# Spectral mixing matmuls of one frequency on 128x32 tiles instead of two frequencies on 128x64 tiles

## The chip, the cores and the metric

The kernel runs on one core of a Trainium2 chip. The metric is the device time of one execution in microseconds (us), as the median of several runs. One further execution was recorded by the hardware profiler; all views of the profile come from it. Engines are named as the profile names them: PE is TensorE (matmuls), PEld its weight loads, DVE VectorE, ACT ScalarE, POOL GpSimd, SP SyncE, which here only issues DMAs.

## The reference

The input x has 16 images of 16 channels of 256x256 numbers in fp32. Two layers are applied, each as "normalise in groups, convolve, add to the input":

```python
x = x + _L0_conv_ref(_gn(x), L0_conv_weight)
x = x + _L1_conv_ref(_gn(x), L1_conv_ty, ..., L1_conv_weights_residue)
```

The first convolution is a circular 3x3 convolution, written with FFTs. The second is a Laplace layer:

```python
alpha = jnp.fft.fft2(x, axes=(-2, -1))
S = jnp.einsum('ikpq,oikp,xikq->oxik', weights_residue, A, Bm)
output_residue1 = jnp.einsum('biox,oxik->bkox', alpha, S)
...
x1 = jnp.fft.ifft2(output_residue1, s=(Ny, Nx), axes=(-2, -1)).real
return x1 + x2 / Nx / Ny
```

S holds, for each of the 256x256 frequencies, a complex 16x16 matrix from input channel i to output channel k. The second einsum mixes the channels with it, frequency by frequency, for all 16 images b. It is this einsum that the change touches. x2, a transient part, is made of a few projections of alpha and of exponentials.

## The kernel before

Everything is fp32. The span has four stages, each with its own pools of SBUF and PSUM tiles, and in each the program order of every engine's instructions is the order in which the Python code issues them (a manual schedule); semaphores keep the data dependencies between engines.

1. To about 640 us: the 3x3 convolution with 32x32 tiles of the PE array (`conv`, L300); its result, folded in y, goes to vD in HBM.
2. To about 1195 us: the transform along y and x by matmuls with cosine and sine tables (L786, L794, L829), and projections (L814). The spectrum goes to aD in HBM: 128 x-frequencies on the first axis, 32 rows (16 channels, real and imaginary), then 256 y-frequencies by 16 images.
3. From 1206 to 1797 us: the mixing stage, which the change touches.
4. From there to the end: the inverse transform, per output channel k and group of four images (L1398 along x, L1422 and L1423 along y), the addition of the input, and the store of the result.

**The mixing stage.** The loop at L1242 takes 32 rounds g of four x-frequencies each. A round has four quarters n (also called jq) of 64 y-frequencies. A moving tile `abd[jq]` holds the spectrum of the four x-frequencies s as a block-diagonal operand: its 128 partitions are 32 rows times four s, and outside the blocks it is zero (memset once; `load`, L1115, writes only the blocks). So one matmul over 128 partitions mixes four x-frequencies at once, and 64 of its columns (four s by 16 images b) belong to one y-frequency. There is one `abd` buffer per quarter, quarters 0 and 1 sharing a tile that one `load` call fills (four DMAs of 256 KB); quarters 2 and 3 take four DMAs of 128 KB each.

The stationary operand `sg` holds S for the round: 128 partitions, 128 pairs of y-frequencies, 32 outputs m (16 channels, real and imaginary), and the two members e of the pair. It is made one round ahead: `sums` (L1036) forms it with matmuls on 64x32 tiles from the weights of `weights` (L904: DVE and POOL), and `spread` (L1060) copies it from PSUM, half of it by an ACT copy, half by a DVE shuffle.

`mix` (L1132) handles 16 y-frequencies per call. One matmul (L1141) takes a pair of them at once: the stationary operand has 64 columns (32 m by 2 e), the moving one 128 columns (2 frequencies o by 4 s by 16 b). The product holds all four combinations of e and o; only those with e = o are wanted. Two column tiles t of 64 columns are used, one for each half of the y-frequencies. A call fills one PSUM tile `ps_mix` (512 columns, one bank, four buffers), which is copied whole to the row tile `yt` (L1265), by ACT for m = 0 and 1, and by DVE for m = 3; m = 2 goes to DVE just after a step of `make_exps` in which ACT loads a table, otherwise to ACT.

A quarter's `yt` (three buffers) is written to yD in HBM by `store` (L1153) in two DMAs, one per e, which pick the wanted half. yD has, for each x-frequency, 64 rows (t and m) of 2048 numbers (e, quarter, then image and frequency), with a gap of 256 numbers after each row. All loads and stores of this stage are issued by SP in program order: per quarter `store(g, n)` and `load(g + 1, n)`, where for n = 1 the load comes first. `make_exps` (L1182) spreads the making of the exponentials for stage 4, mostly POOL work, over the quarters. After round 30, `unmix_first` (L1160) reads back the part of yD with x-frequency 0, separates two frequencies that share it and writes it again.

**The start of stage 4.** `load_images` (L1315) reads the channel-0 part of yD, four images at a time (the first on the POOL queue for 120 partitions and on SP for the last 8; the rest on SP); `load_quarter` (L1337) reads the later channels in quarters, one row of 2048 numbers for each partition. `combine` (L1350, POOL) then forms the operand of the inverse transform.

Of the kernel before, what the change touches and what calls it, by code (L numbers as in the profile page):

```python
# [9 lines left out]
FP = mybir.dt.float32  # L10
# [14 lines left out]
def conv_then_laplace_kernel(ctx: ExitStack, tc: tile.TileContext, a: dict, out: bass.AP):  # L25
# [44 lines left out]
        t = dp.tile([P, C, 8 * N + 256], FP, name=f"vD{b}", tag=f"vD{b}")  # L70
        vD.append(t[:, :, 0 : 8 * N].rearrange("p c (b h x) -> p c b h x", b=4, h=2))
    aD = pitched("aD", 2 * C, N * B)
    yD = pitched("yD", 4 * C, N * B // 2, 2, 4)
    cD = dp.tile([P, 4, 8, N], FP, name="cD", tag="cD")
    hD = dp.tile([7, 2, 16, C * C * 4], FP, name="hD", tag="hD")
    eD = [dp.tile([n, P, C, 2, P], FP, name=f"eD{n}", tag=f"eD{n}") for n in (2, 1)]
# [917 lines left out]
    ptab.close()  # L994


    yp = pool(p2, "yt", 3)
    g0 = pool(p2, "sg0")
    a0 = pool(p2, "abd0")
    wp = pool(p2, "w", 2)  # L1000
# [128 lines left out]
                    out=abd[jq][s::4, s].rearrange("r c j b -> r c (j b)"), in_=src[:, :, jq]  # L1129
                )  # L1130

    def mix(n, sg, yt):  # L1132


        ps = pm.tile([P, 4, 2, 4, B], FP, name="ps_mix", tag="ps_mix")
        jq = n // 4
        for j in range(4):
            cc, jj = divmod(4 * (n % 4) + j, 8)
            for t in range(2):
                f = 128 * t + 64 * cc + 16 * jq + 2 * jj  # L1140
                nc.tensor.matmul(  # L1141
                    ps[64 * t : 64 * t + 64, j],
                    lhsT=sg[:, f // 2].rearrange("p m e -> p (m e)"),
                    rhs=abd[jq][:, :, 2 * t + cc, 2 * jj : 2 * jj + 2].rearrange(
                        "p s j b -> p j s b"
                    ),
                    start=True,
                    stop=True,
                )
        j0 = 4 * (n % 4)  # L1150
        return yt[:, :, :, j0 : j0 + 4], ps.rearrange("p j o s b -> p o (s b) j")

    def store(g, jq, yt):  # L1153
        for e in range(2):
            nc.sync.dma_start(
                out=yD[4 * g : 4 * g + 4, :, e, jq].rearrange("s k n -> k s n"),
                in_=yt[e::2, e].rearrange("p (s b) j -> p s (b j)", s=4),
            )

    def unmix_first():  # L1160

        z2 = new_sg(32).rearrange("p (a n) m e -> p a (n m e)", a=4)[:, 0:2]
        z, t = (z2[:, j, 0:1024].rearrange("p (c n) -> p c n", c=4) for j in range(2))
        at = yD[0]
        for c in range(4):
            nc.sync.dma_start(out=z[:, c], in_=at[32 * (c // 2) : 32 * (c // 2) + 32, c % 2])
        yield
        lo, hi = z[:, 0:2], z[:, 2:4]  # L1170
        nc.vector.scalar_tensor_tensor(t[:, 0:2], hi, osgn, lo, ALU.mult, ALU.add)
        nc.vector.scalar_tensor_tensor(t[:, 2:4], lo, nosgn, hi, ALU.mult, ALU.add)
        nc.vector.tensor_scalar(t, t, 0.5, None, ALU.mult)
        t0, z0 = t[:, 0:3:2, 0:256:16], z[:, 0:3:2, 0:256:16]
        nc.vector.tensor_tensor(z0, z0, t0, ALU.subtract)
        nc.vector.scalar_tensor_tensor(t0, z0, first, t0, ALU.mult, ALU.add)
        for c in range(4):
            nc.sync.dma_start(out=at[32 * (c // 2) : 32 * (c // 2) + 32, c % 2], in_=t[:, c])

    def make_exps(which):  # L1182


        pl = ep.tile([P, C, 2], FP, name="s_pl", tag="s_pl")
        nc.sync.dma_start(out=pl, in_=a[f"pole_e{which + 1}"])
        t = ep.tile([P, N], FP, name="s_t", tag="s_t")
        nc.sync.dma_start(out=t, in_=a[("ty", "tx")[which]].to_broadcast([P, N]))
        most, least = (cols[:, j : j + 1] for j in ((8, 10), (11, 18))[which])
        sign, phase, turns = (cols[:, 2 + 3 * which + j : 3 + 3 * which + j] for j in range(3))  # L1190
        pim = ep.tile([P, C], FP, name="s_pim", tag="s_pim")
        for _ in range(4):
            yield
        nc.gpsimd.tensor_scalar(pim, pl[:, :, 1], sign, None, ALU.mult)
        for q in range(8):
            th = ep.tile([P, 2, N], FP, name="s_th", tag="s_th")
            rn = ep.tile([P, N], FP, name="s_rn", tag="s_rn")
            tmp = ep.tile([P, N], FP, name="s_tmp", tag="s_tmp")
            ex = ep.tile([P, 2, N], FP, name="s_ex", tag="s_ex")
            for j in range(2):  # L1200
                i = 2 * q + j
                nc.gpsimd.tensor_scalar(th[:, j], t, pim[:, i : i + 1], None, ALU.mult)
            magic = 1.5 * 2.0**23
            c1 = 6.28125
            c2 = float(np.float32(1.93500518798828125e-3))
            c3 = 2 * np.pi - c1 - c2
            for j in range(2):
                z = th[:, j]
                nc.gpsimd.tensor_scalar(rn, z, 1.0 / (2 * PI), turns, ALU.mult, ALU.add)
                nc.gpsimd.tensor_scalar(rn, rn, magic, magic, ALU.add, ALU.subtract)  # L1210
                for c in (c1, c2, c3):
                    nc.gpsimd.tensor_scalar(tmp, rn, float(c), None, ALU.mult)
                    nc.gpsimd.tensor_tensor(z, z, tmp, ALU.subtract)
                yield
            nc.gpsimd.tensor_scalar(th, th, most, least, ALU.min, ALU.max)
            for j in range(2):
                i = 2 * q + j
                nc.scalar.activation(ex[:, j], t, AF.Exp, scale=pl[:, i, 0:1])
            yield True
            yield  # L1220
            nc.scalar.activation(th, th, AF.Sin, bias=phase)
            yield True
            nc.gpsimd.tensor_tensor(th, th, ex, ALU.mult)
            for op, eo in ((ALU.add, 0), (ALU.subtract, 1)):
                nc.gpsimd.tensor_tensor(
                    ex[:, :, eo * P : eo * P + P], th[:, :, 0:P], th[:, :, N - 1 : P - 1 : -1], op
                )
            yield
            for o in range(2 - which):
                nc.sync.dma_start(  # L1230
                    out=eD[which][o, :, 2 * q : 2 * q + 2].rearrange("p i e t -> p i (e t)"),
                    in_=ex,
                )
            yield
# [3 lines left out]
    ahead, wt = first_sums(), None  # L1238
    o2 = finish_projections()
    unmix = None  # L1240
    exps, late = chain(make_exps(0), make_exps(1)), None
    for g in range(32):  # L1242
        sg, w_now = ahead, wt
        if g == 0:
            w_now = at_once(weights(1))
            nc.gpsimd.memset(abd[3], 0.0)
            steps = weights(2)
            next(steps)
        ahead = new_sg(g + 1) if g < 31 else None
        for n in range(4):  # L1250
            if g == 0:
                sets = ((), (0,), (1,), (2, 3))[n]
            else:
                sets = (n,) if ahead is not None else ()
            if g == 0:
                banks = {j: sums(j, w_now) for j in sets}
            elif sets and n % 2 == 0:
                banks = {j: sums(j, w_now) for j in (n, n + 1)}
            evict = [banks[j] for j in sets]
            yt = yp.tile([P, 2, 4 * B, 16], FP, name="yt", tag="yt")  # L1260
            for m in range(4):
                for j, ps in zip(sets, evict) if m < 2 else ():
                    spread(j, (ahead, [couples(z) for z in ps]), odds=(m,))
                o, src = mix(4 * n + m, sg, yt)
                (nc.vector.tensor_copy if m >= (2 if late else 3) else nc.scalar.copy)(o, src)  # L1265
            if n == 1 and g < 31:
                load(g + 1, n)
            store(g, n, yt)
            if g == 0 and n == 0:
                load(0, 3)  # L1270
            if n != 1 and g < 31:
                load(g + 1, n)
            if n == 1 and unmix is not None:
                next(unmix, None)
            if n == 3:
                steps = weights(g + 3) if g < 29 else iter(())
            wt = next_step(steps, None) or wt
            late = g and next(exps, None)
        if g == 30:
            unmix = unmix_first()  # L1280
            next(unmix)
# [33 lines left out]
    def load_images(yk, b0, rows, eng):  # L1315

        at = slice(16 * b0, 16 * b0 + 64)
        for r in range(2):
            for h in range(2):
                eng.dma_start(  # L1320
                    out=yk[r][rows, h].rearrange("p c b j -> p c (b j)")[:, :, at],
                    in_=yD[rows, 2 * C * h + C * r].rearrange("p e q n -> p (e q) n")[:, :, at],
                )

    def load_tables(k, eng=nc.gpsimd):
# [11 lines left out]
    def load_quarter(k, n, yk):  # L1337
        r, h = divmod(n, 2)
        nc.sync.dma_start(
            out=yk[r][:, h].rearrange("p c b j -> p (c b j)"),  # L1340
            in_=yD[:, 2 * C * h + C * r + at(k)].rearrange("p e q n -> p (e q n)"),
        )

    def load_v(k, b0):
# [305 lines left out]
```

## Time and profile before

| What | Value |
|---|---|
| Median of 3 runs | 2562.41 us (2560.56 to 2570.66) |
| Profiled execution, its own time | 2559.74 us |
| Its span | 2557.7 us, 83730 instructions |
| Mean granted TensorE clock | 0.99 |
| PE busy | 2446.8 us (96%), 35314 matmul records |
| DVE busy | 1836.5 us (72%) |
| ACT busy | 1433.9 us (56%) |
| POOL busy | 1255.0 us (49%) |
| DMA | 653.11 MB, mean 255 GB/s |

The span is what the profiler saw from the first to the last instruction; the execution's time is 2.0 us longer. Busy shares are averages over four stages with different limits, so a stage has to be read by itself. A group of instructions is given as line, engine, operation, output and inputs, tile of the PE array (rows*columns), shape, count, then the busy time in us, the mean duration of one in ns, and the idle time of the engine just before them with what ended it. An fp32 matmul appears as two records on PE and two on PEld. Records of matmuls that run in different tiles of the array overlap, so busy time (their union) is far below count times mean. Matmul ends are modelled; their starts are recorded.

### The profile page before, as it was taken

The page shows a single profiled execution, that of the slowest core. Times are in us where ns is not written, and L with a number is a line of the kernel's source. Part 1 is how long each engine was busy: PE and PEld are TensorE (multiplying, and loading weights), DVE is VectorE, ACT ScalarE, POOL GpSimd, SP SyncE. Part 2 cuts the span into 40 slices and gives each one's busy share as a digit, 9 for nine tenths or more (in the row PEclk, how much of TensorE's full clock was granted, in tenths as well). Part 3 has the DMA queues.
Part 4 walks back from the last instruction along what each step waited for, and adds up shares of the span by engine and source line. Part 5 has one row for each costly group of instructions (what it writes and reads, how often), then busy time and mean ns, then how long its engine had stood idle before and what let it go on. Part 6 is the DMA issues. An engine that isn't in the chain of part 4 may idle for free. (4 is left out here: it accounts for less than half of the span.)

```text
span 2557.7 us, 83730 instructions
## 1 busy us (share of the span) xinstructions
PE 2446.8 (96%) x35314; PEld 1895.7 (74%) x35314; DVE 1836.5 (72%) x3771; ACT 1433.9 (56%) x2603; POOL 1255.0 (49%) x1277
## 2 busy tenths in 40 slices
PE   4999999999999999998999999999899999999998
PEld 2454555457777777775899999998688888888887
DVE  7777789848888888887566666665367676666766
ACT  2566666675666666665677767776344434444443
POOL 1333369442333333334376756664655655556553
PEclk9999999999999999999999999999899999999999
DMA  7889878865456456456777777777988888889884
GB/s 272 271 292 300 280 264 292 289 239 201 189 224 247 194 218 247 194 219 216 230 255 248 255 253 246 243 244 247 278 286 292 293 291 283 294 282 306 282 290 167
DMA packets 314070, 653.11 MB, mean 255 GB/s; under 512 B 45238, under 2 KB 160054, under 8 KB 301792
## 3 DMA queue, kind: packets, MB, share of 16 engines
q1 hardware_dynamic: 312720, 644.23, 73.2%
q8 instruction: 278, 4.55, 0.7%
q0 software_dynamic: 928, 3.02, 0.5%
q10 hardware_dynamic: 48, 0.52, 0.2%
q14 instruction: 96, 0.79, 0.1%
HBM read 368.15 MB, written 280.36 MB: 254 GB/s over the span
## 5 line engine op out<-in xcount | busy, mean ns | idle before, releaser
L1362 POOL TENSOR_TENSOR u<-yk 128x512 f32<-128x512 f32 (+1 forms) x268 | 351.7, 1345 | 313.8 <-PE ps_p L1398 243.9
L300 PE MATMUL ps_conv<-xt,wc 32*32 32x512 f32 x12288 | 447.2, 606 | 30.5 <-issue 21.0
L1141 PEld LDWEIGHTS ps_mix<-abd,sg 128*64 128x64 f32 x8192 | 446.8, 137 | 36.7 <-issue 30.0
L1141 PE MATMUL ps_mix<-abd,sg 128*64 128x128 f32 x8192 | 463.4, 274 | 9.2 <-DVE yt L1265 4.9
L300 PEld LDWEIGHTS ps_conv<-xt,wc 32*32 32x32 f32 x12288 | 252.3, 104 | 212.5 <-issue 117.7
L802 ACT ACTIVATE t<-ps_y,vmr 128x384 f32<-128x384 f32 x512 | 296.8, 580 | 156.6 <-PE ps_y L794 156.4
L786 PE MATMUL ps_y<-tabE,vq 128*128 128x256 f32 x1024 | 313.3, 388 | 1.8 <-ACT t L802 1.8
L794 PE MATMUL ps_y<-tabO,vq 128*128 128x256 f32 x1024 | 305.9, 380 | 0.0
L1422 PE MATMUL ps_f<-pt,inv 128*128 128x256 f32 x1008 | 300.5, 380 | 0.0
L1423 PE MATMUL ps_f<-hs,ey 128*128 128x256 f32 x1008 | 299.8, 379 | 0.0
L271 POOL TENSOR_TENSOR pair<-pair,far 128x1024 f32<-128x1024 f32 x64 | 151.7, 2370 | 297.2 <-DVE pair L268 195.5
L1398 PEld LDWEIGHTS ps_p<-inv,u 128*128 128x128 f32 x2048 | 268.6, 193 | 35.3 <-POOL u L1366 11.4
L1398 PE MATMUL ps_p<-inv,u 128*128 128x128 f32 x2048 | 276.2, 278 | 9.9 <-POOL u L1366 9.8
L1426 DVE TENSOR_TENSOR r<-ps_f,q 128x256 f32<-128x256 f32 x256 | 106.9, 418 | 245.0 <-ACT q L1425 224.1
L1265 ACT COPY yt<-ps_mix 128x512 f32<-128x512 f32 x352 | 203.2, 586 | 110.6 <-PE ps_mix L1141 39.4
L1425 ACT COPY q<-ps_f 128x256 f32<-128x256 f32 x256 | 95.4, 372 | 273.9 <-PE ps_f L1423 250.4
L786 PEld LDWEIGHTS ps_y<-tabE,vq 128*128 128x128 f32 x1024 | 189.5, 191 | 78.6 <-ACT q L842 50.3
L1265 DVE COPY yt<-ps_mix 128x512 f32<-128x512 f32 x160 | 108.9, 688 | 180.8 <-PE ps_mix L1141 175.4
L1400 ACT COPY pt<-ps_p 128x512 f32<-128x512 f32 x256 | 151.5, 592 | 137.1 <-PE ps_p L1398 137.1
L666 POOL TENSOR_TENSOR vq<-vf 128x512 f32<-128x512 f32 x63 | 80.1, 1272 | 289.8 <-DVE vf L670 278.8
L1066 ACT ACTIVATE sg<-ps_s,mcol 128x512 f32<-128x512 f32 (+1 forms) x264 | 178.5, 677 | 68.8 <-PE ps_s L1043 30.0
L794 PEld LDWEIGHTS ps_y<-tabO,vq 128*128 128x128 f32 x1024 | 195.5, 191 | 26.8
(243 smaller groups left out, 4037.0 us busy)
## 6 DMA issues: line engine op xcount, KB each, us to landing
xt<-in_x SPq DMA_DIRECT2D x288, 258.0 KB
vD<-pair SPq DMA_DIRECT2D x256, 256.0 KB
yD<-yt SPq DMA_DIRECT2D x256, 256.0 KB
vl<-vD SPq DMA_DIRECT2D x128, 512.0 KB
out_y<-ol SPq DMA_DIRECT2D x128, 512.0 KB
s<-vD SPq DMA_DIRECT2D x124, 512.0 KB
aD<-spec SPq DMA_DIRECT2D x15, 4096.0 KB
yk<-yD SPq DMA_DIRECT2D x60, 1024.0 KB
```

Of the source, the lines that this page charges most:

```text
L271: nc.gpsimd.tensor_tensor(lo, lo, hi, ALU.subtract)
L300: nc.tensor.matmul(acc[r][32 * c : 32 * c + 32], lhsT=ready[b][0][rows, phase, tap], rhs=halves[b][u // 2][rows, q : q + 5 : 4, 2 - tap : ...
L786: nc.tensor.matmul(ps[:, 0:N], lhsT=vf[:, xo, 0, j], rhs=tabE[:, 0 : i + 2 : i + 1], start=True, stop=False, skip_group_check=True,)
L794: nc.tensor.matmul(ps[:, P : P + N], lhsT=vf[:, xo, 1, j], rhs=tabO[:, i : C + 1 : C - i], start=False, stop=True, skip_group_check=True,)
L802: nc.scalar.activation(t[:, xo, j].rearrange("p l n -> p (l n)"), ps[:, 0:384], AF.Copy, scale=vmr[:, 0, b0 + j, i : i + 1],)
L1066: nc.scalar.activation(columns_of(to, k), src[odd], AF.Copy, scale=nsgn)
L1141: nc.tensor.matmul(ps[64 * t : 64 * t + 64, j], lhsT=sg[:, f // 2].rearrange("p m e -> p (m e)"), rhs=abd[jq][:, :, 2 * t + cc, 2 * jj : 2 ...
L1265: (nc.vector.tensor_copy if m >= (2 if late else 3) else nc.scalar.copy)(o, src)
L1362: nc.gpsimd.tensor_tensor(u[:, :, j].rearrange("p b (c n) -> p c b n", c=8), in0, in1, o)
L1398: nc.tensor.matmul(ps[:, at], lhsT=u[:, n], rhs=tab, start=True, stop=True)
L1422: nc.tensor.matmul(ps[:, e], lhsT=tab, rhs=pt[:, e], start=True, stop=False)
L1423: nc.tensor.matmul(ps[:, e], lhsT=ey[:, e], rhs=hs, start=False, stop=True)
```

## The change

Each mixing matmul takes one y-frequency: 32 stationary columns (the m of one e, every second number of `sg`), 64 moving columns, and one of four column tiles c = (t, e) of 32 columns. Every product is wanted. There are twice as many matmuls, each with half the columns in both operands. A call of `mix` now covers 32 y-frequencies in one PSUM tile of 512 columns, so there are two calls a quarter instead of four. ACT copies the first, DVE the second; the flag that moved a copy to DVE is gone. `yt` is half as large and has six buffers; one `store` of 128 partitions writes it. yD has 128 rows (c and m) of 1024 numbers (quarter, image, frequency) with the same gap of 256. The readers of yD follow: `load_images` has four DMAs for each of two parts where it had two, `load_quarter` reads two pieces of 1024 numbers for each partition, and `unmix_first` addresses the new rows. Block-diagonal operands, `sums`, `spread`, the loads of `abd` and the order of loads and stores stay.

```diff
-    yD = pitched("yD", 4 * C, N * B // 2, 2, 4)
+    yD = pitched("yD", 8 * C, N * B // 4, 1, 4)[:, :, 0]
...
-    yp = pool(p2, "yt", 3)
+    yp = pool(p2, "yt", 6)
...
-    def mix(n, sg, yt):
-        ps = pm.tile([P, 4, 2, 4, B], FP, name="ps_mix", tag="ps_mix")
-        jq = n // 4
-        for j in range(4):
-            cc, jj = divmod(4 * (n % 4) + j, 8)
-            for t in range(2):
-                f = 128 * t + 64 * cc + 16 * jq + 2 * jj
+    def mix(n, cc, sg, yt):
+        ps = pm.tile([P, 8, 4, B], FP, name="ps_mix", tag="ps_mix")
+        for j in range(8):
+            for c in range(4):
+                t, e = divmod(c, 2)
                 nc.tensor.matmul(
-                    ps[64 * t : 64 * t + 64, j],
-                    lhsT=sg[:, f // 2].rearrange("p m e -> p (m e)"),
-                    rhs=abd[jq][:, :, 2 * t + cc, 2 * jj : 2 * jj + 2].rearrange(
-                        "p s j b -> p j s b"
-                    ),
+                    ps[32 * c : 32 * c + 32, j],
+                    lhsT=sg[:, 64 * t + 32 * cc + 8 * n + j, :, e],
+                    rhs=abd[n][:, :, 2 * t + cc, 2 * j + e],
                     start=True,
                     stop=True,
                 )
-        j0 = 4 * (n % 4)
-        return yt[:, :, :, j0 : j0 + 4], ps.rearrange("p j o s b -> p o (s b) j")
+        return yt[:, :, 8 * cc : 8 * cc + 8], ps.rearrange("p j s b -> p (s b) j")

     def store(g, jq, yt):
-        for e in range(2):
-            nc.sync.dma_start(
-                out=yD[4 * g : 4 * g + 4, :, e, jq].rearrange("s k n -> k s n"),
-                in_=yt[e::2, e].rearrange("p (s b) j -> p s (b j)", s=4),
-            )
+        nc.sync.dma_start(
+            out=yD[4 * g : 4 * g + 4, :, jq].rearrange("s k n -> k s n"),
+            in_=yt.rearrange("p (s b) j -> p s (b j)", s=4),
+        )
...
-            yt = yp.tile([P, 2, 4 * B, 16], FP, name="yt", tag="yt")
-            for m in range(4):
-                for j, ps in zip(sets, evict) if m < 2 else ():
+            yt = yp.tile([P, 4 * B, 16], FP, name="yt", tag="yt")
+            for m in range(2):
+                for j, ps in zip(sets, evict):
                     spread(j, (ahead, [couples(z) for z in ps]), odds=(m,))
-                o, src = mix(4 * n + m, sg, yt)
-                (nc.vector.tensor_copy if m >= (2 if late else 3) else nc.scalar.copy)(o, src)
+                o, src = mix(n, m, sg, yt)
+                (nc.vector.tensor_copy if m else nc.scalar.copy)(o, src)
...
-            for h in range(2):
+            for c in range(4):
+                h, e = divmod(c, 2)
                 eng.dma_start(
-                    out=yk[r][rows, h].rearrange("p c b j -> p c (b j)")[:, :, at],
-                    in_=yD[rows, 2 * C * h + C * r].rearrange("p e q n -> p (e q) n")[:, :, at],
+                    out=yk[r][rows, h, 4 * e : 4 * e + 4].rearrange("p c b j -> p c (b j)")[:, :, at],
+                    in_=yD[rows, 2 * C * c + C * r][:, :, at],
                 )
...
         nc.sync.dma_start(
-            out=yk[r][:, h].rearrange("p c b j -> p (c b j)"),
-            in_=yD[:, 2 * C * h + C * r + at(k)].rearrange("p e q n -> p (e q n)"),
+            out=yk[r][:, h].rearrange("p (e c) b j -> p e (c b j)", e=2),
+            in_=yD[:, 4 * C * h + C * r + at(k) :: 2 * C][:, 0:2].rearrange("p e q n -> p e (q n)"),
         )
```

More of the change, by code (lines that the diff above doesn't have):

```diff
@@ L1167, in unmix_first @@
         for c in range(4):
-            nc.sync.dma_start(out=z[:, c], in_=at[32 * (c // 2) : 32 * (c // 2) + 32, c % 2])
+            nc.sync.dma_start(out=z[:, c], in_=at[32 * c : 32 * c + 32])
         yield
@@ L1177, in unmix_first @@
         for c in range(4):
-            nc.sync.dma_start(out=at[32 * (c // 2) : 32 * (c // 2) + 32, c % 2], in_=t[:, c])
+            nc.sync.dma_start(out=at[32 * c : 32 * c + 32], in_=t[:, c])
     def make_exps(which):
@@ L1218, in make_exps @@
                 nc.scalar.activation(ex[:, j], t, AF.Exp, scale=pl[:, i, 0:1])
-            yield True
+            yield
             yield
             nc.scalar.activation(th, th, AF.Sin, bias=phase)
-            yield True
+            yield
             nc.gpsimd.tensor_tensor(th, th, ex, ALU.mult)
@@ L1240, in conv_then_laplace_kernel @@
     unmix = None
-    exps, late = chain(make_exps(0), make_exps(1)), None
+    exps = chain(make_exps(0), make_exps(1))
     for g in range(32):
@@ L1277, in conv_then_laplace_kernel @@
             wt = next_step(steps, None) or wt
-            late = g and next(exps, None)
+            if g:
+                next(exps, None)
         if g == 30:
```

## The prediction

> **What bounds the kernel now.** I read the 40 slices first, then the costliest groups, then the time line of TensorE through one round of the mixing stage, then the engines' windows. The changed code runs from 1206 to 1797 us, slices 19 to 28.
>
> The page, busy tenths in 40 slices of 64 us:
>
> ```profile
> PE   4999999999999999998999999999899999999998
> ...
> DMA  7889878865456456456777777777988888889884
> ```
>
> TensorE is full all through, the stage of interest included; the DMA engines stand at seven tenths there. Next the groups (line, engine, operation, count, then busy us, mean ns, idle before):
>
> ```profile
> L1141 PE MATMUL ps_mix<-abd,sg 128*64 128x128 f32 x8192 | 463.4, 274 | 9.2 <-DVE yt L1265 4.9 <-issue 2.3 <-DMA abd<-aD 1.6
> L300 PE MATMUL ps_conv<-xt,wc 32*32 32x512 f32 x12288 | 447.2, 606 | 30.5 <-issue 21.0 <-ACT pair L319 5.7 <-DVE wc L244 3.7
> ...
> L1265 ACT COPY yt<-ps_mix 128x512 f32<-128x512 f32 x352 | 203.2, 586 | 110.6 <-PE ps_mix L1141 39.4 <-ACT sg L1066 24.8 <-DMA abd<-aD 21.6
> ...
> L1265 DVE COPY yt<-ps_mix 128x512 f32<-128x512 f32 x160 | 108.9, 688 | 180.8 <-PE ps_mix L1141 175.4 <-issue 2.1 <-DMA yD<-yt 1.6
> ...
> L1382 PE MATMUL ps_h<-et,o 32*32 32x256 f32 x2048 | 55.4, 392 | 4.7 <-DVE r L1427 4.7
> ...
> L814 PE MATMUL psd<-t,hB 128*32 128x128 f32 x1024 | 42.9, 279 | 0.3 <-ACT t L802 0.3
> ```
>
> The mixing matmuls idle 9 us in 463, and the copies wait for them, not they for the copies. One fp32 matmul is two records: 4096 matmuls, 8192 rows. The time line of TensorE (start, length) gives one round g:
>
> ```profile
> 1240.87 1.96 PE L1043 MATMUL ps_s<-ct,w 64*32 64x256 f32 x64
> 1242.76 7.21 PE L1141 MATMUL ps_mix<-abd,sg 128*64 128x128 f32 x128
> 1249.89 1.96 PE L1043 MATMUL ps_s<-ct,w 64*32 64x256 f32 x64
> 1251.78 7.21 PE L1141 MATMUL ps_mix<-abd,sg 128*64 128x128 f32 x128
> 1258.92 0.88 PE L1043 MATMUL ps_s<-ct,w 64*32 64x256 f32 x24
> ```
>
> A round is 1258.92 - 1240.87 = 18.05 us with no gap: twice 1.88 us of sums and 7.14 us of mixing (55.8 ns a record). The windows of that stage (us, then busy us and instructions of PE, PEld, DVE, ACT, POOL, then clock, DMA share, GB/s):
>
> ```profile
> 1400.00:1500.00 100.00, 100.00 (x2128) 90.12 (x2126) 65.45 (x163) 73.15 (x121) 67.68 (x75) 1.00 0.79 253
> ```
>
> So TensorE is the bound. Behind it, per round: DMA 14.0 us at its mean share of 0.775, ACT 13, POOL 12, DVE 11.8.
>
> [...] matmul records in different column tiles start 6 to 14 ns apart. [...] the mixing stage moves 248 on average and 370 in its busiest 4 us.
>
> **The mixing matmuls.** Now a pair of column tiles streams 128 columns and takes 2 x 55.8 = 111.6 ns. After, four column tiles stream 64 columns each, twice as many matmuls (8192, 16384 records). If streaming sets the pace, a group of four takes half the pair's time, 56 ns, or 14 ns a record: 16384 x 14 = 229 us for 463. Weights need not slow it: a load record takes 190 ns for 128 columns, 137 for 64, 106 for 32, so 27 ns per 32 columns over a constant, and loads of different column tiles overlap. Line 814 is the same tile shape with 128 columns: in one burst its records start at 0, 13, 26, 40, 133, 146, 160, 173, 242 ns, so four per 109 ns, all four tiles at full speed.
>
> What no row shows for long is the rate of instructions: four per matmul (two loads, two matmuls), so one per 7 ns. The nearest is a burst of line 1382 that had just waited (PE, then PEld, of that line alone):
>
> ```profile
> 2522.28:2522.53 0.25, 0.25 (x30) 0.24 (x28) 1.00 0.93 377
> ```
>
> 58 instructions in 0.25 us are 4.3 ns each, a matmul per 17 ns. The other end is line 300, where records come every 447.2 / 12288 = 36.4 ns; but 512 columns on 16 tiles need 26.7 of that for streaming, and its PSUM and ACT waits are in it. Bounds: 14 to 36 ns a record; I take 14 to 15, since the burst shows the supply and line 814 the tiles. TensorE's round becomes 2 x (1.88 + 256 x 14 ns) = 2 x 5.46 = 10.9 us.
>
> **What takes over.** Copies: 512 become 256, 128 on each engine. ACT loses 224 x 586 ns = 131 us, DVE 32 x 688 = 22 us; both have slack today, so this is worth nothing by itself, but leaves ACT 9 and DVE 11.2 us a round. POOL keeps its 11.8. SP: a round issues 12 loads and 8 stores at 0.60 us, 12.1 us; after, 12 and 4, some 9.7 us (a 128-row store at 0.6; if it took 1.2, 12.1). Bytes are unchanged, 4.19 MB a round besides the tables, so DMA keeps 14.0 us of work and becomes the longest. abd has one buffer: quarters 0 and 1 (1 MB) are loaded once mixing of quarter 1 ends, needing some 2.4 us of issue, 3.3 of transfer, and queueing; yet the other stores and loads of the round are issued without waiting for that load, so the engines have about 8 us of work queued when it lands, against 3.7 us until the next is issued. DMA can run without a hole. At 4.19 + 0.25 MB and 300 to 370 GB/s the round is 12.0 to 14.8 us; I take **14.2 us**. Gain in 30 steady rounds: 30 x (18.05 - 14.2) = 115.5 us.
>
> Round 0 (1206.3 to 1240.9) has 14.6 us of mixing among waits for POOL, ACT and loads: half of the 7 us saved, 4 us. Round 31 ends through the unmixing of frequency 0 (a load, five DVE operations, four stores, with the last yD stores behind them on SP). The 4.95 us for which TensorE waits there on a copy go with six yt tiles, but SP's chain stays: 1 us.
>
> **The last stage.** Its start is exposed: the stores land at 1799.5 us, then the first images are read through four POOL issues (0.93 us each for 960 pieces; 128-piece ones take 0.54) and SP. Eight of half the pieces take about 0.70 each: +1.9 us; SP's first group doubles from 1.34 us, and 12 further issues become 24: they took 1.6 us each with 1024 pieces, held by the queue, so pieces, not counts, set them. I take **+3 us** (bounds 0 and 10). Then quarters of yk arrive in 4 KB pieces for 8 KB ones. In this trace a 4 KB piece takes 174 ns and an 8 KB one 454, so it costs nothing, and TensorE covers it (496.6 of 500 us busy); without that cover 60 loads would show a few us at most. The steadier alternation of copies and the dropped flag around the table loads cost ACT at most a wait that four PSUM banks hide.
>
> Sum, against the profiled execution: 2559.7 - 115.5 - 4 - 1 + 3 = 2442 us. The median of the runs shown is 2.7 us above that execution, so I predict 2445.
>
> **Rivals.**
> 1. *Instruction supply sets the pace* (slower). Twice the records at line 300's 36.4 ns: 16384 x 36.4 = 596 us against 463, so about 2695 us. It decides from 463.4 / 16384 = 28.3 ns a record on. For it: no row of the page is below 27 ns a record (line 1382: 55.4 / 2048), and instructions are fetched by the same DMA engines that I expect to be full. Against: the burst, and that those rows hold short bursts with their tails.
> 2. *A floor in between.* [...] about 2515. The same comes out if [...] the single abd buffer leaves holes in the queue.
> 3. *DMA is no bound.* TensorE, DVE and POOL at about 11.8 us: 30 x 6.25 = 188 us, about 2375.
> 4. *Hidden anyway*: excluded as long as TensorE is full; it comes back only as an exact tie of 1 or 2 with today, 2550 to 2575.
>
> **Chances.** My forecast 0.50 (its own range 2405 to 2485), rival 2 0.16, rival 3 0.09, a tie 0.05, rival 1 0.20. So 0.75 faster, 0.05 within 0.5% (13 us, about what a measurement of this kernel can tell from no change), 0.20 slower. The range reaches from half of rival 3 to the near edge of rival 1: 2385 to 2600.
>
> **What would show it.** Right: 16384 mixing records at 14 to 18 ns each while they run; rounds of about 14 us; TensorE below full in slices 19 to 26, its idle time ended by abd<-aD; DMA share near 1, around 300 GB/s or more; 128 copies each on ACT and DVE; the last stage's 46 us steps unchanged. Wrong: TensorE still full with mixing above 500 us (rival 1); rounds of 16 to 17 us [...] (rival 2); DMA share below 0.85 while TensorE waits for abd (holes); the first images of the last stage later by over 10 us after the last yD store.

## The result, and the profile after

The changed kernel takes 2669.28 us (median of 5 runs, 2664.34 to 2675.37); the kernel before, run beside it, 2561.17 us (2555.77 to 2570.66). The ratio is 1.042, with a 95% interval of 1.039 to 1.045. The forecast of 2445 us and its range were wrong, and so was the sign: what came is rival 1, that the supply of instructions sets the pace.

The page after: engines and DMA in 40 slices of 67 us (busy tenths, then GB/s), then the DMA queue that carries instructions (packets, MB, share of 16 engines). The mixing stage lies in slices 18 to 28.

```profile
PE   5999999989999999996666666666699999999998
...
DMA  7888888755565556546666666666888888888884
GB/s 268 274 292 292 286 275 306 263 212 202 195 253 230 197 206 245 226 173 226 201 209 213 214 213 204 205 217 200 221 319 291 293 296 284 285 293 286 301 283 177
...
q8 instruction: 343, 5.62, 0.9%
```

TensorE is no longer full in the stage, at six or seven tenths, and the DMA engines, which the forecast had made the new bound, are less busy than before: about 210 GB/s for 250. Both engines that were to be the bound wait.

The costliest groups of TensorE and the copies after, every shape by itself (line, engine, operation, tile, shape, count, then busy us, mean ns, idle before with what ended it):

```profile
L300 PE MATMUL ps_conv<-xt,wc 32*32 32x512 f32 x12288 | 450.1, 603 | 29.8 <-issue 22.1 <-DVE wc L244 3.7 <-ACT pair L319 3.6
...
L1139 PE MATMUL ps_mix<-abd,sg 128*32 128x64 f32 x16384 | 306.8, 235 | 214.8 <-issue 211.2 <-DMA abd<-aD 3.3 <-DVE sg L1098 0.2
...
L1259 ACT COPY yt<-ps_mix 128x512 f32<-128x512 f32 x128 | 75.0, 586 | 275.4 <-PE ps_mix L1139 182.5 <-issue 85.8 <-DMA abd<-aD 4.9
L1259 DVE COPY yt<-ps_mix 128x512 f32<-128x512 f32 x128 | 88.4, 691 | 292.2 <-PE ps_mix L1139 289.6 <-DMA abd<-aD 2.2
```

The mixing matmuls are busy for 307 us, 157 less than before, and stand still for 215 where they stood 9. 211 of these are put down to "issue": nothing that the profile shows was awaited, neither data (3.3 us for abd) nor a free PSUM bank. The time line of TensorE in one stretch of the stage (start, length, count, idle before) gives this a shape:

```profile
1500.82 2.00 PE L1139 MATMUL ps_mix<-abd,sg 128*32 128x64 f32 x128 [0.99 <-issue]
1504.29 0.98 PE L1139 MATMUL ps_mix<-abd,sg 128*32 128x64 f32 x52 [1.48 <-issue]
1505.19 1.96 PE L1043 MATMUL ps_s<-ct,w 64*32 64x256 f32 x64
1507.08 0.36 PE L1139 MATMUL ps_mix<-abd,sg 128*32 128x64 f32 x9
1508.02 2.00 PE L1139 MATMUL ps_mix<-abd,sg 128*32 128x64 f32 x127 [0.58 <-issue]
1512.85 1.89 PE L1139 MATMUL ps_mix<-abd,sg 128*32 128x64 f32 x120 [2.83 <-issue]
```

While they run, the matmuls are as fast as forecast: 128 records in 2.00 us, of which the last takes 0.22, so 14.0 ns from record to record. Then TensorE stops for 0.6 to 2.8 us. From stop to stop it runs some 128 records: 52 + 64 + 9 = 125 is about the same count across two kinds of matmul. With the weight loads, as many records again, and the semaphore instructions among them, that is 256 instructions: of the 98 distances between the 99 stops over 0.6 us from 1260 to 1800 us, 96 are 256, 512 or 768 instructions exactly.

The engines' windows in that stage say the same (us, then busy us and instructions of PE, PEld, DVE, ACT, POOL, then clock, DMA share, GB/s):

```profile
1400.00:1500.00 100.00, 65.26 (x2912) 51.73 (x2900) 49.25 (x125) 41.41 (x65) 57.56 (x66) 0.90 0.67 215
```

5812 TensorE instructions in 100 us, for 4254 before: 17.2 ns each. The faster matmuls bought a third more instructions in the same time, but the change needs 1280 a round where there were 768, two thirds more.

Where the time went, by stages of the two profiled executions (their spans differ by 104.9 us): mixing from its first to its last matmul takes 698.3 us for 587.4, 110.9 more; from there to the end 760.0 for 764.0, 4 less; what lies before, 2 less.

### The profile page after: what moved, and what is told of

It is laid out like the page before. It is cut to its first block, busy times and chain, and to the rows that moved or that the text cites. A ratio compares the mean times of both kernels' runs of the same rounds, so it can differ in the third digit from the quotient of the medians.

```text
span 2662.6 us, 99892 instructions
## 1 busy us (share of the span) xinstructions
PE 2327.6 (87%) x43506; PEld 1731.6 (65%) x43506; DVE 1816.0 (68%) x3739; ACT 1320.5 (50%) x2379; POOL 1265.4 (48%) x1281
## 4 chain that ended last, share of the span: by engine, by line
PE 75%; issue 10%; DVE 7%; DMA 6%; SPq 2%; ACT 1%; POOL 1%; DVEq 0%; ACTq 0%; POOLq 0%
PE ps_mix L1139 11%; PE ps_conv L300 10%; PE ps_y L786 9%; PE ps_y L794 8%; PE ps_p L1394 7%; PE ps_f L1418 7%; PE ps_f L1419 7%; PE ps_s L1043 6%; PE ps_x L829 4%; PE ps_h L1378 2%; DMA vD<-pair 2%; PE psd L814 1%; DMA xt<-in_x 1%; DVE r L1427 1%; DVE ol L1429 1%
## 5 line engine op out<-in xcount | busy, mean ns | idle before, releaser
L1358 POOL TENSOR_TENSOR u<-yk 128x512 f32<-128x512 f32 (+1 forms) x268 | 358.2, 1370 | 299.5 <-PE ps_p L1394 238.7
L1139 PE MATMUL ps_mix<-abd,sg 128*32 128x64 f32 x16384 | 306.8, 235 | 214.8 <-issue 211.2
L1139 PEld LDWEIGHTS ps_mix<-abd,sg 128*32 128x32 f32 x16384 | 275.5, 120 | 263.7 <-issue 260.1
L1259 DVE COPY yt<-ps_mix 128x512 f32<-128x512 f32 x128 | 88.4, 691 | 292.2 <-PE ps_mix L1139 289.6
L1066 ACT ACTIVATE sg<-ps_s,mcol 128x512 f32<-128x512 f32 (+1 forms) x264 | 173.0, 675 | 129.8 <-PE ps_s L1043 100.1
L1259 ACT COPY yt<-ps_mix 128x512 f32<-128x512 f32 x128 | 75.0, 586 | 275.4 <-PE ps_mix L1139 182.5
```

Of the source, the lines that this page charges most:

```text
L1066: nc.scalar.activation(columns_of(to, k), src[odd], AF.Copy, scale=nsgn)
L1139: nc.tensor.matmul(ps[32 * c : 32 * c + 32, j], lhsT=sg[:, 64 * t + 32 * cc + 8 * n + j, :, e], rhs=abd[n][:, :, 2 * t + cc, 2 * j + e], s ...
L1259: (nc.vector.tensor_copy if m else nc.scalar.copy)(o, src)
L1358: nc.gpsimd.tensor_tensor(u[:, :, j].rearrange("p b (c n) -> p c b n", c=8), in0, in1, o)
```

## What the stops are

The queue q8 carries 343 packets of 16.4 KB; before it carried 278 (0.7% of the 16 engines' span). TensorE's matmuls and weight loads are 2 x 43506 after and 2 x 35314 before, 254 to a packet both times, and with its semaphore and drain instructions the trace has 87964 and 71342, 256 to 257 to a packet. So the packets of q8 hold blocks of 256 TensorE instructions, and their times in the trace's DMA records can be set beside the stops. The DMA view of the 400 us from 1300 to 1700, kernel before:

```profile
q8 instruction: 67, 1.10, 1.1%
```

and after:

```profile
q8 instruction: 93, 1.52, 1.6%
```

Before, a block lasts 5.97 us on average; after, 4.30 us. Five blocks of 4.30 us are the 21.5 us of a round after (178 copies of sg, eight a round, in 480 us: 21.6 us). In the DMA records of the changed kernel, a block lands, and TensorE goes on 1.39 us later (median of the 99 stops; eight of ten lie between 1.26 and 1.55). The next fetch starts 1.48 us after that (median, most between 1.1 and 2.7), and takes 1.0 us. The medians add up to some 3.9 us from block to block, and 99 of 100 fetches of the stage start at least 3.37 us after the one before. Counted on in steps of 256 instructions, TensorE enters 93 blocks from 1300 to 1700 us, each 1.1 to 2.4 us after it has landed, and the next fetch starts 0.8 to 4.4 us after that, one to a block: in this stage one block is fetched ahead. By an estimate from these medians, a block that runs for longer than some 4 us hides its successor's fetch (before, at 5.97 us a block, TensorE has no wait on issue in these 400 us), and one that runs for 2 us pays the other 2.

## The experiments

My theory after this reading (S): the supply of TensorE instructions. The rivals: the 128x32 tile shape itself, with its weights picked with a step (T); waits for DMA and the single abd buffer (D); and the lower granted clock of the stage, 0.90 to 0.92. In the comparisons, "before" always ran beside the experiment.

**More instructions, and nothing else.** The kernel before, in which each mixing matmul is cut into two of 64 columns on its old 128x64 tile. Layout, copies, stores and the columns streamed stay.

```diff
-            for t in range(2):
+            for o in range(2):
+              for t in range(2):
...
-                    ps[64 * t : 64 * t + 64, j],
+                    ps[64 * t : 64 * t + 64, j, o],
...
-                    rhs=abd[jq][:, :, 2 * t + cc, 2 * jj : 2 * jj + 2].rearrange(
-                        "p s j b -> p j s b"
-                    ),
+                    rhs=abd[jq][:, :, 2 * t + cc, 2 * jj + o],
...
```

> The kernel before with every mixing matmul cut in two of 64 moving columns on its 128x64 tile: the same products, copies, stores and streaming time (four records of 64 columns for two of 128), but 8192 mixing matmuls instead of 4096, as in the changed kernel. Theory S (TensorE is short of instructions: it fetches them in blocks of 256, one block per 4.27 us in the changed kernel's mixing stage): a round has 1280 PE instructions in place of 768, so 21.4 us and more in place of 18.05, in all 2660 to 2700 us, with idle time put down to issue between runs of 128 mixing records. Theory T (the 128x32 tile shape or its stepped weights are slow): no 128x32 tile here, so as before, 2555 to 2570 us.

Measured: 2669.01 us (2659.25 to 2675.13), ratio 1.0415 (1.039 to 1.044), the time of the changed kernel within 0.3 us. Its group of mixing matmuls and its window:

```profile
L1142 PE MATMUL ps_mix<-abd,sg 128*64 128x64 f32 x16384 | 512.7, 223 | 52.7 <-issue 47.9 <-DMA abd<-aD 2.2 <-ACT sg L1066 1.6
```

```profile
1400.00:1500.00 100.00, 93.71 (x3002) 83.79 (x3000) 54.81 (x138) 60.22 (x101) 57.47 (x66) 1.00 0.66 212
```

The instructions of 100 us are again about 6000 (6002; 5812 after), again 93 packets of q8 in the 400 us. Only two tiles share the array here and not four, so 64 columns keep it busy for twice as long and less of the time shows as idle, but the pace is the same. Not all of it is stops: within runs a record starts every 29.7 ns, where half of the old 55.8 would be 27.9, which is some 0.9 of the 3.7 us by which a round grows (an estimate from the record starts). The tile shape (T) is out as the cause, and so is the clock: it is 1.00 here. What costs 4% is the count of instructions.

**Fewer instructions on the new tiles.** The changed kernel with 16 matmuls of 128 columns in a PSUM tile instead of 32 of 64; it leaves out half of the products. Everything else, the transfers too, is as after.

```diff
-        for j in range(8):
+        for j in range(0, 8, 2):
...
-                    ps[32 * c : 32 * c + 32, j],
+                    ps[32 * c : 32 * c + 32, j : j + 2],
...
```

> The changed kernel with 16 mixing matmuls of 128 moving columns in place of each 32 of 64, on the same 128x32 tiles; every second frequency is mixed with its neighbour's weights, so half the products are left out, while copies, stores, loads and layouts stay. Theory S: 768 PE instructions a round as before the change, 12.8 us of supply, so the DMA engines' 14 us decide, rounds of 14 to 15 us and 2410 to 2460 us in all. Theory T: records still stall in this tile shape, 2550 us or more. Theory D (DMA waits or the single abd buffer, not instructions, hold the rounds at 22 us): rounds stay above 20 us, 2600 us or more.

Measured: 2490 us (one run). The group and a window of the stage:

```profile
L1139 PE MATMUL ps_mix<-abd,sg 128*32 128x128 f32 x8192 | 260.9, 280 | 58.0 <-issue 41.1 <-DMA abd<-aD 10.8 <-ACT sg L1066 5.3
```

```profile
1400.00:1500.00 100.00, 78.76 (x2432) 63.56 (x2424) 68.19 (x173) 57.73 (x93) 67.65 (x75) 0.97 0.90 288
```

With the count of instructions back at 768 a round, the stage is 15.7 us a round instead of 21.6, so the supply it is. But it missed the expected 2410 to 2460. The 14.2 us for which the forecast took the DMA engines are not reached: they stand at 0.90 and 288 GB/s, and TensorE waits in turn for instructions (41.1 us in the mixing matmuls), abd (10.8) and, in the sums, for DVE (21.7) and POOL (15.7). Even with as few instructions as before, then, the gain is some 30 x (18.05 - 15.7) = 70 us, not 115; what it would be with no stop on issue at all was not measured.

**Does other traffic slow the fetches?** The changed kernel, in which abd is loaded for round 0 only; later rounds mix stale data.

```diff
-        if jq == 0:
+        if jq == 0 or g > 0:
             return
```

> The changed kernel without the loads of abd after round 0, so that all rounds mix the first round's data; half the bytes of the mixing stage are left out, its instructions on PE are the same. Theory D: rounds fall to the 12 us of the other engines, 2350 us. Theory S with a fetch time of its own: fetches stay near 4.2 us a block, within 2620 to 2670 us. Theory S with fetches slowed by the data traffic on the same DMA engines: blocks come every 3.4 us (the least seen) to 3.8 us, rounds of 17 to 19 us, 2500 to 2570 us.

Measured: 2597.39 us (one run), with 103 packets of q8 in the 400 us, 3.88 us a block, at 124 GB/s:

```profile
L1139 PE MATMUL ps_mix<-abd,sg 128*32 128x64 f32 x16384 | 280.0, 224 | 168.4 <-issue 167.5 <-DMA abd<-aD 0.6 <-DVE sg L1098 0.2
...
q8 instruction: 103, 1.69, 1.7%
```

Between the two expectations. Without the loads a block comes 0.4 us sooner. That is little of a block, and of the other 3.9 us these loads are no part. But it is 2 us a round, of some 3.5 that the change had cost, and 72 of its 108 us: without these loads two thirds of the loss are gone. And D is out as the whole cause: with no loads to wait for, the kernel is still slower than before.

**The matmuls without the new layout.** The kernel before with all four quarters on single frequencies and 128x32 tiles, two copies a quarter, but the old yD, its readers and its two stores (of 64 adjoining partitions).

```diff
+    ONE = (0, 1, 2, 3)
...
-                in_=yt[e::2, e].rearrange("p (s b) j -> p s (b j)", s=4),
+                in_=(yt[64 * e : 64 * e + 64, 0] if jq in ONE else yt[e::2, e]).rearrange("p (s b) j -> p s (b j)", s=4),
...
-            for m in range(4):
+            for m in range(2 if n in ONE else 4):
...
+                if n in ONE:
+                    o, src = mix1(n, m, sg, yt)
...
```

> The kernel before with the changed matmuls alone: one frequency on 128x32 tiles, PSUM tiles of 512 columns copied half by ACT and half by DVE, but yD, its readers and the two stores a quarter as before, and yt in three buffers of full size. Theory S: all of the loss comes with the matmuls, 2655 to 2675 us. If the new rows of yD, the single store or the readers caused it: 2440 to 2560 us.

Measured: 2697.56 us (2696.81 to 2706.85), ratio 1.053 (1.051 to 1.055). The group, and the instruction packets from 1300 to 1700 us:

```profile
L1158 PE MATMUL ps_mix<-abd,sg 128*32 128x64 f32 x16384 | 313.6, 238 | 226.0 <-issue 222.0 <-DMA abd<-aD 3.3 <-ACT sg L1066 0.4
q8 instruction: 89, 1.46, 1.5%
```

The matmuls alone bring all of the loss and more. The last 28 us over the changed kernel were not expected: a block takes 4.49 us here, at a DMA share of 0.70 for 0.67. Besides its two stores, this kernel differs from the changed one in the old yD and in three yt tiles of full size; which of these slows the fetches was not tested.

**The layout without the matmuls.** yD in 128 rows and all its readers as after; matmuls, PSUM tiles, copies and two stores as before.

```diff
-    yD = pitched("yD", 4 * C, N * B // 2, 2, 4)
+    yD = pitched("yD", 8 * C, N * B // 4, 1, 4)[:, :, 0]
...
```

> The rest of the change alone: yD in 128 rows of 1024 numbers with its readers, the mixing matmuls, PSUM tiles, yt and two stores a quarter as in the kernel before (rows of yD in the order e, t, m). Theory S, which puts all of the loss on the number of PE instructions: same as before within 10 us, 2552 to 2572 us, with mixing rounds of 18.05 us. If the new rows of yD cost anything in the last stage it shows here as more than 10 us.

Measured: 2558.45 us, ratio 1.0002 (0.9991 to 1.0013). Halved pieces, 20 more issues at the start of the last stage (8 on POOL for 4, 32 on SP for 16) and the smaller first reads cost nothing that can be measured.

**One quarter on single frequencies.** If blocks matter and not matmuls, part of the change could pay: on the new layout, with quarter 3 alone (and two rings of two yt tiles), a round has 896 instructions (3.5 blocks), 18.4 ns for each in a round of 16.5 us.

```diff
+    ONE = (3,)
...
-            for m in range(4):
+            for m in range(2 if n in ONE else 4):
...
+                if n in ONE:
+                    o, src = mix(n, m, sg, yt)
+                else:
+                    o, src = mix2(4 * n + m, sg, yt)
```

> A mixture: quarter 3 of every round takes one frequency each on 128x32 tiles with one store, quarters 0 to 2 take pairs on 128x64 tiles as before. 896 PE instructions a round. Theory S with one block of 256 fetched ahead, each taking about 4.3 us or the block's own matmul time if that is longer: 15.0 us of supply against 16.4 us of matmuls, of which a part does not overlap: rounds of 16.5 to 17.3 us and 2505 to 2545 us in all, faster than both kernels. Theory T (tile shape): slower than before, since each 128x32 quarter takes longer than a pair quarter and each change of shape is added, 2570 us or more.

Measured: 2555.18 us (2546.67 to 2569.24), ratio 0.998 (0.9958 to 0.9994). A miss: the gain is some 0.2%. The profiled execution, at 2569.0 us one of the slowest, has rounds of 18.0 us. What TensorE waited for from 1300 to 1700 us (engine and tile, line, cause, us in total, times, longest):

```profile
PE ps_s L1045 <- issue: 9.7, 8, 1.9
PE ps_mix L1141 <- issue: 5.8, 5, 2.1
PE ps_s L1045 <- DVE sg L1071: 3.4, 5, 2.1
```

**Two quarters on single frequencies**, 1 and 3: 1024 instructions, four blocks a round.

```diff
-    ONE = (3,)
+    ONE = (1, 3)
```

> The same mixture with quarters 1 and 3 on 128x32 tiles: 1024 PE instructions a round, four blocks of 4.3 us, 17.2 us of supply against 14.7 us of matmuls. Theory S: rounds of 17.2 to 18.5 us, 2530 to 2575 us, no better than one quarter. Theory T: slower than one quarter by as much as that one is slower than before.

Measured: 2561.01 us, ratio 1.0001 (0.9988 to 1.0014). The instruction packets from 1300 to 1700 us:

```profile
q8 instruction: 88, 1.44, 1.5%
```

That is 4 x 4.55 = 18.2 us a round, the 18.05 of before within 1%. Four blocks at what the fetches give is about the round that the streaming of before takes, so this is a tie.

**Did order on DVE and the yt tiles take the gain of one quarter?** The kernel with quarter 3, with the DVE shuffles for its sums moved a quarter earlier and one ring of three yt tiles.

```diff
-    yp = pool(p2, "yt", 3 if not ONE else 2)
-    yp1 = pool(p2, "yt1", 2)
+    yp = pool(p2, "yt", 3)
...
+                    now = [(2 + m // 2, banks[2 + m // 2], m % 2)] if n == 2 else []
```

> As the run with quarter 3 alone on single frequencies (896 TensorE instructions a round), with two things changed: from the second round on the DVE shuffles of quarter 3 are issued in quarter 2 and not between the copies and the weights step of quarter 3, and the results' tiles are one ring of three. If that run lost its gain to those two waits (DVE and yt), rounds come to 16.4 to 17.2 us for 18.05 and the time to 2510 to 2545 us. If the supply of instructions took it (896 instructions at 19 ns or more a round, fetches still at 4.3 us or more on average with TensorE idle on issue), it stays at 2550 to 2560 us whatever the order on DVE. If the earlier shuffles put TensorE's other waits out of step, it is above 2560 us.

Measured: 2554.97 us (2545.88 to 2567.31), ratio 0.9976 (0.9964 to 0.9988). The waits for DVE are gone and "issue" has taken their place (20.4 us in the same 400):

```profile
PE ps_s L1044 <- issue: 13.6, 11, 2.6
PE ps_mix L1140 <- issue: 5.1, 5, 2.7
PE ps_mix L1156 <- issue: 1.7, 3, 1.0
```

One round of its time line:

```profile
1363.52 1.96 PE L1044 MATMUL ps_s<-ct,w 64*32 64x256 f32 x64
1365.41 3.71 PE L1156 MATMUL ps_mix<-abd,sg 128*64 128x128 f32 x64
1369.05 2.00 PE L1140 MATMUL ps_mix<-abd,sg 128*32 128x64 f32 x128
1370.98 0.63 PE L1044 MATMUL ps_s<-ct,w 64*32 64x256 f32 x6
1374.14 1.94 PE L1044 MATMUL ps_s<-ct,w 64*32 64x256 f32 x58 [2.53 <-issue]
1376.01 7.21 PE L1156 MATMUL ps_mix<-abd,sg 128*64 128x128 f32 x128
```

Here the average supply is no limit: 79 packets came in 400 us where the changed kernel got 93. But quarter 3 (256 instructions in 1.9 us) and the sums behind it (128 in 1.9 us) make 384 fast instructions in a row. As 896 instructions are 3.5 blocks, in about every second round they hold a whole block, which runs in 1.9 to 2.9 us, and that block's successor is late; in the others the stops are mostly smaller (0.24 us in the round before this one).

**The same instructions, with the bursts apart.** Quarter 1 is the single one, and the second half of the sums stands in the middle of quarter 2.

```diff
-    ONE = (3,)
+    ONE = (1,)
...
-            elif sets and n % 2 == 0:
-                banks = {j: sums(j, w_now) for j in (n, n + 1)}
+            elif sets and n == 0:
+                banks = {j: sums(j, w_now) for j in (0, 1)}
...
+                    if n == 2 and m == 2:
+                        banks = {j: sums(j, w_now) for j in (2, 3)}
+                    j = {(0, 0): 0, (0, 2): 1, (2, 2): 2, (3, 0): 3}.get((n, m // 2 * 2))
+                    now = [] if j is None else [(j, banks[j], m % 2)]
```

> The same 896 TensorE instructions a round as the last run, in another order: quarter 1 is the one on single frequencies, and the second half of the sums stands in the middle of quarter 2, so that the 256 fast instructions of quarter 1 have paired quarters before and behind them and no stretch of fast instructions is longer than 256 (384 in the last run: quarter 3 and the sums behind it). If TensorE starves because only one block of 256 is fetched ahead, so that a burst drains it though the average of 18.4 ns an instruction could be supplied, the stalls on issue go from 1.4 us a round to under 0.5 us, rounds come to 16.5 to 17.1 us and the time to 2510 to 2535 us. If the average supply is what limits (fetches can't come faster than every 5 us beside this traffic), the time stays at 2550 to 2560 us.

Measured: 2530.96 us (2530.46 to 2532.59) for 2562.72 of before beside it, ratio 0.988 (0.986 to 0.990). TensorE's waits from 1300 to 1700 us fell from 20.4 to 3.3 us:

```profile
PE ps_mix L1156 <- issue: 3.1, 6, 0.9
PE ps_s L1044 <- issue: 0.2, 1, 0.2
```

and two of its rounds show when a stop remains:

```profile
1404.38 3.71 PE L1156 MATMUL ps_mix<-abd,sg 128*64 128x128 f32 x64
1408.02 1.99 PE L1140 MATMUL ps_mix<-abd,sg 128*32 128x64 f32 x128
1409.94 0.32 PE L1156 MATMUL ps_mix<-abd,sg 128*64 128x128 f32 x1
1411.13 1.97 PE L1156 MATMUL ps_mix<-abd,sg 128*64 128x128 f32 x31 [0.87 <-issue]
...
1422.19 3.71 PE L1156 MATMUL ps_mix<-abd,sg 128*64 128x128 f32 x64
1425.84 2.00 PE L1140 MATMUL ps_mix<-abd,sg 128*32 128x64 f32 x128
1427.77 1.97 PE L1156 MATMUL ps_mix<-abd,sg 128*64 128x128 f32 x32
```

In the first round TensorE stops one record after the burst, so the burst nearly fills a block; in the next, half a block later, it is split over two blocks with slow matmuls around it, and nothing stops. It is the fastest kernel of this study that forms every product, 1.2% faster than before.

**The order alone.** The last kernel with all quarters on pairs.

```diff
-    ONE = (1,)
+    ONE = ()
```

> The last run's order of work (second half of the sums in the middle of quarter 2, shuffles issued half a quarter earlier) with all four quarters on paired frequencies: 768 TensorE instructions a round, the order alone. If the last run gained by the single-frequency quarter, this stays within 0.5% of before, 2550 to 2570 us, with rounds of 18.0 us, since TensorE has no gap in the rounds of before. If the order itself brought the gain, it comes to 2525 to 2540 us.

Measured: 2563.16 us, ratio 1.0013 (1.0002 to 1.0025). The new order alone brings no gain. It pays only with the narrower matmuls, and those of one quarter brought 0.2% without it.

The kernels side by side. Rounds are from the copies of sg, eight a round, counted over 480 us; us per block is 400 us over the packets of q8 between 1300 and 1700 us:

| Kernel | Instructions a round | us per block | Round, us | Time, us |
|---|---|---|---|---|
| before | 768 | 5.97 | 18.0 | 2561 |
| order alone | 768 | 5.97 | 17.9 | 2563 |
| quarter 1 single, bursts apart | 896 | 4.82 | 17.1 | 2531 |
| quarter 3 single, shuffles earlier | 896 | 5.06 | 17.8 | 2555 |
| two quarters single | 1024 | 4.55 | 18.3 | 2561 |
| after | 1280 | 4.30 | 21.6 | 2669 |
| before, matmuls cut in two | 1280 | 4.30 | 21.7 | 2669 |

Shown by these: the count of TensorE instructions sets the loss, and their order within a few hundred decides at equal count. That the stops are fetches rests on the block count between stops and on the times of q8's packets; no run changed the fetching itself.

## Why the prediction was wrong, point by point

**The tiles: right.** Four 128x32 tiles stream at once; a record starts every 14.0 ns while they run, as forecast from line 814. Inside a group of four tiles the starts mostly lie 6 to 7 ns apart, and about 36 ns lie between groups. The floor of rival 2 was an assumption of the author's and was not shown: records start every 14.0 ns across four tiles, and rounds take 21.6 us for its 16 to 17.

**The supply: the step that failed.** "I take 14 to 15, since the burst shows the supply and line 814 the tiles". The burst of line 1382 shows nothing of the kind. It had just waited, and the last packet of q8 before it had landed almost 8 us earlier (2514.5 us), so its 58 instructions were there already; they are less than a quarter of one block. What was wanted is a rate over several blocks. Measured, it is 4.30 us for 128 records, 33.6 ns a record over mixing and sums together, near the bound that was set aside. 640 records at that are 21.5 us, where the forecast had 10.9.

Rival 1 named the mechanism and, at 2695, came 26 us from the time. Its price of 36.4 ns a record was near by luck, since line 300 has other waits in it; but that line's own entry, 21.0 us of idle time put down to "issue", was the sign of a shortage in the profile of before, and the forecast counted it as if it were a tail. The DMA records of before show it: of that line's 29 stops over 0.1 us, 21, with 21.3 of 30.4 us, end 1.1 to 1.65 us after a packet of q8 has landed, as the stops of the changed kernel do. Of the two reasons given against the rival, the burst was no evidence, and "short bursts with their tails" was no explanation of 21 us on "issue". Of the reasons for it, that fetches share the DMA engines with the data was sound: the loads taken away, a block came only 0.4 us of 4.3 sooner, but that was two thirds of the loss (one run). The profile of before had the blocks (278 packets, 256 to 257 instructions each); the forecast did not ask how fast one can follow another. From 1300 to 1700 us TensorE has no wait where blocks of the kernel before come every 5.97 us, waits 3.3 us on issue with the bursts apart (4.82 us a block), and 134.3 us in the changed kernel (4.30).

**DMA as the next bound: the work right, the round not reached.** 14.2 us a round was taken. With the instructions halved the round is 15.7 us at a DMA share of 0.90, which is 14.1 us of work for the engines, near the 14.0 of the forecast. That the round comes down to this work is not shown: stops on issue and waits among the sums are still in it, and no run separates them.

**Copies and stores: right in size, without effect.** 128 copies each on ACT (586 ns) and DVE (691 ns, 688 taken), none on the path; issuing a store took 0.37 us (median; 0.6 taken).

**The last stage: small, as forecast.** +3 us were taken with bounds of 0 and 10. The stretch from the last mixing matmul to the end became 4 us shorter, but two experiments that keep the changed kernel's last stage have 761 and 773 us for its 760, so 4 us say little. With the layout alone the stretch is as long as before (764.0 us), and the time changes by 0.02%.

**The signs named beforehand.** Records at 14 ns, and TensorE below full: both came. Rounds of 14 us, idle time ended by abd, and a DMA share near 1 did not. For rival 1 the prediction expected TensorE full with mixing above 500 us: 306.8 us busy and 214.8 idle are 522 us, but a shortage of instructions shows as idle time on "issue" where each instruction is short, and as busy time where it is long (the kernel with its matmuls cut in two: 512.7 busy, 52.7 idle).

## What to carry to other kernels

Count TensorE instructions as well as columns: an fp32 matmul is four here (the 8192 mixing matmuls left 16384 records and as many weight loads), so 64 matmuls are one block of 256, and in this kernel a block that runs in less than about 4 us leaves TensorE waiting (an estimate from 1.39 + 1.48 + 1.0 us). Here making matmuls narrower paid only for one quarter in four (1.2%), and what counted was the block, not the average: with the burst of quarter 1 between slow matmuls, the waits on issue in 400 us fell from 20.4 us to 3.3 at the same count. "Issue" idle after runs of 128 matmul records, and the packets of the instruction queue, are how a profile shows it; the rate of a burst shorter than a block (58 instructions at 4.3 ns) said nothing on the rate over blocks (16.8 ns an instruction).

## What was not expected of the hardware

Undisturbed by the loads, a block of 256 TensorE instructions still takes 3.9 us, though its packet is on the DMA engines for only about 1.0: 1.39 us pass from its landing to the next matmul, and 1.34 (median, most between 1.1 and 1.9) until the next fetch begins. With the loads the first two are the same; only the next fetch begins later (1.48). Two mixing kernels with the same instruction count but other stores and tiles for the results had 4.30 and 4.49 us a block. And the granted clock of 0.90 in the starved stage was not the cause: at 1.00 the same count of instructions took the same time. What lowers it stays open: without the loads TensorE was as idle (67% busy from 1500 to 1600 us), at a clock of 1.00.
